# Masks made between the first graph's steps, a last group in two halves, and a longer wait before an input is turned

## The chip, the cores and the metric

The kernel runs on one core of a Trainium2 chip. The metric is the device time in microseconds of one execution. The profile's span, from the first to the last instruction, is a little shorter than that time.

## The reference

Eight graphs share one adjacency matrix of 2048 nodes; each node has 256 channels. For every graph the program computes masked attention in 8 heads of 32 channels, a feed-forward block, and three layer normalizations:

```python
qkv = x @ w_qkv                                    # (F=8, N=2048, 3*256)
scores = einsum('fnhd,fmhd->fhnm', q, k) / sqrt(32)
attn = softmax(where(adj > 0, scores, -1e9))
t = attn @ v
x1 = layernorm(x + t) * g1 + b1
f_out = relu(x1 @ w1 + b1) @ w2 + b2
ref = layernorm(x1 + f_out) * g2 + b2
out = layernorm(x + ref)
```

The adjacency is an int32 matrix in HBM.

## The kernel before, in words

A **graph** f has four chunks of 512 queries (qc), two groups of four heads (g) and 16 key blocks of 128 (mb). One **item** (f, qc, g, mb) is a key block against 512 queries in four heads; there are 1024 items, 128 for a graph, in the order of the loops f, qc, g, mb. A **group** is the 16 items of one (f, qc, g).

The main loop has a **step** t for each item. It lets the planner run (`advance(t)`), then emits the exponential of item t+1 on ACT (L237), the scores of item t+2 on PE with two additions of the mask on DVE (L230, L233), the values of item t on PE (L249), and `add_up`, which sums exponentials for the softmax denominators. Of the 16 tiles of exponentials of a group, POOL adds six to the first of its chain (L271), and six go by accumulating DMAs issued by POOL (`MOVED`, L268). `denominator` then multiplies the four sums by a block of ones on PE (L315). Scores use three pairs of PSUM banks in turn, values one bank; one more bank is left for all other work.

All other work runs as **generators in a list, sorted by a due time**. In one step at most one generator is given the free bank (`yield BANK`), and a matmul costs credit: 2200 credits come in each step and none are kept over, a projection's half costs 2048, a set of four transposes 1400. A generator that has said `MORE` or `WAIT` keeps the bank. `yield n` sleeps n steps. The generators are: `turn` (loads 512 rows of the next graph's x, L172, sleeps 5 steps, transposes them and stores the result to HBM, L177), `ask` and `project` (reload a transposed chunk, L196, and make queries, or keys and values), `denominator`, `outcome` (division by the denominators, L356, and adding x by a DMA), `tail` (normalizations, feed-forward, output). `NEXT` says at which step of a graph each starts. Inputs use a pool of three tiles, `take` and `give`.

**Masks.** Before the loop, `begin()` reads the adjacency in 16 blocks of 512x512 (qc, c), turns them with PE transposes into fp8 masks (0 or a large negative number, L145, L147) and stores them to HBM (`MD`, L148). After the blocks of qc = 0 and 1 it emits the scores of items 0 and 1; then it makes the blocks of qc = 2 and 3, and then the main loop starts. During the second group of each chunk, at its odd steps, `load_mask` brings the next chunk's masks back from HBM (L151).

**The end.** The very last group's denominators use more, shorter terms. After the last item, `finish` divides, and takes the four rows of the chunk in two interleaved halves (`half_rows`, L396 to L441) through the normalizations and the feed-forward block. A check of the sums (L836 to L848) follows.

An engine executes its instructions in the order in which they are emitted. SP issues the loads and stores; a wait of one of them holds the ones behind it.

Of the kernel before, what the change touches and what calls it, by code (L numbers as in the profile page):

```python
# [10 lines left out]
F32 = mybir.dt.float32  # L11
# [50 lines left out]
def fast_path(ctx, tc, cst, x, adj, out, RS):  # L62
# [62 lines left out]
    MK = {}  # L125
# [23 lines left out]

    def load_mask(f, qc, k):  # L150
        nc.sync.dma_start(words(mask_piece(f, qc, k)), MD[qc, k])  # L151
# [17 lines left out]
    def turn(f, c):  # L169
        yield INPUTS - 2  # L170
        xc, xT = take([P, TPC, C], F32), take([P, 2, CH], F32)
        nc.sync.dma_start(xc, x[f, c * CH:(c + 1) * CH, :].rearrange("(j p) c -> p j c", p=P))  # L172
        yield 5
        yield from turn_rows(xc, xT)
        give(xc)
        yield 1
        nc.sync.dma_start(XD[f][c], xT)  # L177
        XT[f, c] = xT
        give(xT)
# [39 lines left out]

    PT, O, OT, RC, DT = {}, {}, {}, {}, {}  # L220

    def scores(item):
        f, qc, g, mb = item
        pt = PT[item] = pp.tile([P, 4, CH], F32, name="p")
        ps2 = [score_pair() for _ in range(2)]

# [14 lines left out]
    def values(item):  # L241
        f, qc, g, mb = item
        grp = (f, qc, g)
        if mb == 0:
            i = state["side"]
            O[grp] = ps_x[i].tile([P, CH], F32, name=f"x{i}")
# [14 lines left out]
    ENDED = MB - 5  # L261
    SUM = 4

    def add_up(item):
        f, qc, g, mb = item
        for chain in MOVED:
            if mb in chain[1:] and not ((f, qc, g) == items[-1][:3] and mb >= ENDED):
                nc.gpsimd.dma_start(PT[f, qc, g, chain[0]], PT.pop(item), accum_op=ALU.add)  # L268
        if mb in POOLED[1:] and not ((f, qc, g) == items[-1][:3] and mb >= ENDED):
            first = PT[f, qc, g, POOLED[0]]  # L270
            nc.gpsimd.tensor_tensor(first, first, PT.pop(item), ALU.add)  # L271


# [23 lines left out]
    def denominator(f, qc, g, ready):  # L297
# [3 lines left out]
        if (f, qc, g) == items[-1][:3]:  # L301
            blocks = [POOLED[0], 11, 12, MOVED[0][0], 13, 14, MOVED[1][0], 15]
            late = {n: len(items) - k for n, k in ((2, 2), (3, 1), (4, 1), (5, 0), (6, 0), (7, 0))}
# [28 lines left out]
        start(begin, outcome(f, qc) if (f, qc) != (F - 1, NCK - 1) else finish(f, qc), begin)  # L332

    def outcome(f, qc):
# [4 lines left out]
        yield from divide(f, qc, y)  # L339
        nc.gpsimd.dma_start(y, xin, accum_op=ALU.add)  # L340
        begin = items.index((f, qc, 1, LAST)) + SUM + 2
        if (f, qc) == (F - 1, NCK - 2):
            xb = take([P, TPC, C], F32)
            nc.sync.dma_start(xb, xin)
            start(begin + 8, tail(f, qc, y, xin, 2, xb), begin + 11)
# [14 lines left out]
    def tail(f, qc, y, xin, per=1, xb=None):  # L360
# [6 lines left out]
        yield from norm(z, per)  # L367
# [28 lines left out]
    def half_rows(h, y, xr, xb, yT, hT, dst):  # L396
        own = slice(2 * h, 2 * h + 2)
        q = slice(2 * h * P, 2 * (h + 1) * P)
        y, xr, xb = y[:, own], xr[:, own], xb[:, own]
# [3 lines left out]

        nc.vector.tensor_tensor(y, y, xr, ALU.add)
        if h:
            yield
        found = half_stats(y)
        yield
# [3 lines left out]
        yield  # L412
        ps = bank()
        transposes(ps, [y[:, j, a * P:(a + 1) * P] for a in range(2) for j in range(2)])
        for a in range(2):
            nc.scalar.activation(yT[:, a, q], ps[:, a * 2 * P:(a + 1) * 2 * P], AF.Identity,
                                 bias=cst["be1c"][:, a:a + 1], scale=cst["g1c"][:, a:a + 1])
        yield
        ps = bank()
        for d in range(2):  # L420
            for a in range(2):
                columns(ps[:, d * 2 * P:(d + 1) * 2 * P], w1s[:, a, d * P:(d + 1) * P], yT[:, a, q], start=(a == 0), stop=(a == 1))
            nc.scalar.activation(hT[:, d, q], ps[:, d * 2 * P:(d + 1) * 2 * P], AF.Relu, bias=cst["b1s"][:, d:d + 1], scale=1.0)  # L423
        yield
        ps = bank()
        for j in range(2):
            for d in range(2):
                columns(ps[:, j * C:(j + 1) * C], hT[:, d, (2 * h + j) * P:(2 * h + j + 1) * P], w2s[:, d, :],
                        start=(d == 0), stop=(d == 1))
# [3 lines left out]
        yield  # L433
        half_norm(z, *found)
        yield
# [3 lines left out]
        yield  # L439
        half_norm(z, *found)  # L440
        nc.sync.dma_start(dst[:, own], z)  # L441

    def finish(f, qc):
        y = yp.tile([P, TPC, C], F32, name="y")
        xr, xb = state["rows"]
        yield from divide(f, qc, y)
        yT, hT = (work.tile([P, 2, CH], F32, name=n) for n in ("turned", "hT"))
        dst = out[f, qc * CH:(qc + 1) * CH, :].rearrange("(p j) c -> p j c", p=P)
        both = [half_rows(h, y, xr, xb, yT, hT, dst) for h in range(2)]
        while both:  # L450
            for e in list(both):
                if next(e, both) is both:
                    both.remove(e)
            yield 1
# [101 lines left out]

    def begin():
        todo = deque((qc, c) for qc in range(NCK) for c in range(NCK))
# [46 lines left out]
    state["side"] = 0  # L605
    for t, (f, qc, g, mb) in enumerate(items):
        if g == 1 and mb % 2 and (f + 1 < F or qc + 1 < NCK):
            load_mask(f + (qc + 1) // NCK, (qc + 1) % NCK, mb // 2)
        for what, *which in NEXT.get(t % FRAME, []):
# [4 lines left out]
        if t == len(items) - MB // 2:  # L614
            xr, xb = state["rows"] = [take([P, TPC, C], F32) for _ in range(2)]
            nc.sync.dma_start(xr, x[f, qc * CH:(qc + 1) * CH, :].rearrange("(p j) c -> p j c", p=P))
        if t == len(items) - 2:
# [17 lines left out]
        if t == len(items) - 3:  # L635
            start(t, denominator(f, qc, g, t), t)
# [245 lines left out]
```

## Time and profile before

| | |
|---|---|
| median of 3 runs | 3190.41 us (3189.46 to 3194.38) |
| the profiled execution | 3196.28 us, span 3194.5 us |
| mean granted TensorE clock | 0.987 |
| PE, DVE, ACT, POOL busy | 96%, 86%, 76%, 81% of the span |
| DMA | 589.46 MB, mean 185 GB/s |
| span by stage | first additions of masks at 60.1 us; the second step's additions at 98.7; graph 1 begins at 458.9, then graphs 1 to 7 take 391.7, 379.4, 381.2, 381.2, 381.2, 381.2 us, and the last 385.4 us to its last additions |

The stages are read from the starts of the DVE additions (L233) in the timeline, two for each item. A page's group line has the line, the engine, the operation, output and inputs, shapes and count, then busy time, the mean ns of one, and the idle time of the engine before them with what ended it. A PE that is shown busy isn't PE at its peak, since matmuls are pipelined. A line of the timeline has the start, the time taken, the engine, the line, the operation and its count, and in brackets the idle time before it and what ended it.

### The profile page before, as it was taken

Reading aid. Unit: us, or ns where it says so; the run is one execution under the profiler, and the core shown is the slowest. Engines: PE = TensorE matmul, PEld = TensorE weight load, DVE = VectorE, ACT = ScalarE, POOL = GpSimd, SP = SyncE. Lnnn points to the kernel's source line nnn. Section 1 sums busy time; section 2 is a strip of 40 time slices with the busy share of each in tenths; the row PEclk is TensorE's granted clock in tenths of the full one; section 3 lists DMA queues with packets and bytes.
Section 4 is the critical chain, followed back from the end, with each engine's and each line's share of the span. In section 5 each row is a group of like instructions: output and inputs, shape, how many; then the busy total and the mean of one; then the engine's idle time right before and its main releaser. Section 6 shows DMA issues by size and latency. Waiting matters only on the chain. (4 is left out here: it accounts for less than half of the span.)

```text
span 3194.5 us, 68226 instructions
## 1 busy us (share of the span) xinstructions
PE 3081.7 (96%) x28868; PEld 963.0 (30%) x28868; DVE 2749.6 (86%) x3139; ACT 2417.7 (76%) x1909; POOL 2593.3 (81%) x1361
## 2 busy tenths in 40 slices
PE   7899999999999999999999999999999999999985
PEld 4222333222332223332333323323233233332222
DVE  4798988888889988889988988988988888889985
ACT  3677778777787777788777788778778778777774
POOL 0578888788888888888888888888889788889875
PEclk8899999999999999999999999999999999999998
DMA  9688889788798888898888899888879788888872
GB/s 323 142 192 193 183 175 199 161 188 189 179 195 188 191 194 178 176 204 196 187 177 174 194 208 198 168 182 196 196 174 203 177 196 192 176 177 166 178 150 64
DMA packets 153096, 589.46 MB, mean 185 GB/s; under 512 B 15024, under 2 KB 67760, under 8 KB 103888
## 3 DMA queue, kind: packets, MB, share of 16 engines
q0 software_dynamic: 64128, 433.22, 68.8%
q1 hardware_dynamic: 87840, 150.50, 13.7%
q8 instruction: 228, 3.74, 0.4%
q10 hardware_dynamic: 816, 1.31, 0.1%
q14 instruction: 84, 0.69, 0.1%
HBM read 146.67 MB, written 37.75 MB: 58 GB/s over the span
## 5 line engine op out<-in xcount | busy, mean ns | idle before, releaser
L233 DVE TENSOR_TENSOR p<-s,mask 128x1024 f32<-128x1024 f32 x2048 | 2409.1, 1218 | 325.0 <-PE s L230 182.9
L237 ACT ACTIVATE p<-p 128x2048 f32<-128x2048 f32 x1024 | 1956.0, 1910 | 566.5 <-DVE p L233 481.1
L271 POOL TENSOR_TENSOR p<-p 128x2048 f32<-128x2048 f32 x382 | 1875.4, 4909 | 359.1 <-ACT p L237 358.8
L230 PE MATMUL s<-qT,kT 32*128 32x512 f32 x8192 | 1172.5, 642 | 44.2 <-DVE p L233 39.4
L249 PE MATMUL x<-p,v 128*32 128x512 f32 x8192 | 1093.5, 606 | 4.6 <-ACT p L237 4.6
L230 PEld LDWEIGHTS s<-qT,kT 32*128 32x128 f32 x8192 | 320.9, 183 | 671.3 <-DVE p L233 643.6
L268 POOL DMA_DIRECT2D p<-p x382 | 416.8, 1092 | 70.1 <-ACT p L237 46.4
L249 PEld LDWEIGHTS x<-p,v 128*32 128x32 f32 x8192 | 161.5, 108 | 784.0 <-issue 310.2
L315 PE MATMUL x<-p,halves 128*32 128x512 f32 x2080 | 269.9, 595 | 0.0
L54 PE MATMUL x<-in,wqkv 128*32 128x512 f32 x1888 | 245.7, 592 | 0.0
L290 ACT ACTIVATE y<-y,nb,rs 128x256 f32<-128x256 f32 x372 | 219.1, 591 | 6.1 <-POOL nb L287 5.9
L278 DVE BATCH_NORM_STATS2 st<-y 128x6 f32<-128x256 f32 x372 | 155.0, 417 | 1.8 <-POOL y L370 1.8
L54 PE MATMUL x<-turned,w1s 128*32 128x512 f32 x992 | 123.9, 593 | 0.0
L54 PE MATMUL x<-w2s,hT 128*32 128x256 f32 x2016 | 121.8, 382 | 0.0
L54 PEld LDWEIGHTS x<-wqkv,in 128*32 128x32 f32 x3584 | 102.2, 110 | 64.1 <-issue 55.9
L54 PE MATMUL x<-wqkv,in 128*32 128x128 f32 x3584 | 117.4, 273 | 0.0
L315 PEld LDWEIGHTS x<-p,halves 128*32 128x32 f32 x2080 | 67.9, 111 | 156.9 <-issue 155.5
L368 POOL TENSOR_TENSOR y<-y,g2r 128x1024 f32<-128x1024 f32 x31 | 101.6, 3278 | 6.4 <-ACT y L290 6.4
L54 PEld LDWEIGHTS x<-in,wqkv 128*32 128x32 f32 x1888 | 61.3, 110 | 141.3 <-issue 116.5
L284 POOL TENSOR_TENSOR rs<-rs,mhalf 128x4 f32<-128x4 f32 x93 | 96.3, 1035 | 7.8
L370 POOL TENSOR_TENSOR y<-y,be2r 128x1024 f32<-128x1024 f32 x30 | 94.6, 3155 | 0.4
L54 PEld LDWEIGHTS x<-w2s,hT 128*32 128x32 f32 x2016 | 65.9, 111 | 70.7 <-issue 38.5
(121 smaller groups left out, 1301.1 us busy)
## 6 DMA issues: line engine op xcount, KB each, us to landing
p<-p POOLq DMA_DIRECT2D x382, 1024.0 KB, 10.0
in<-xd SPq DMA_DIRECT2D x87, 512.0 KB, 8.9
mask<-md SPq DMA_DIRECT2D x248, 128.0 KB, 8.6
y<-in_x_dram POOLq DMA_DIRECT2D x61, 512.0 KB, 10.1
p<-in_adj_dram SPq DMA_DIRECT2D x16, 1024.0 KB, 9.3
out_dram<-y SPq DMA_DIRECT2D x31, 512.0 KB, 6.2
in<-in_x_dram SPq DMA_DIRECT2D x30, 512.0 KB, 10.6
xd<-in SPq DMA_DIRECT2D x28, 512.0 KB, 8.8
```

Source lines behind the costliest of these rows:

```text
L54: nc.tensor.matmul(out[r:r + D], lhsT[:, r:r + D], rhs, start=start, stop=stop)
L230: nc.tensor.matmul(ps2[half][:, j, :], KT[f, mb // TPC, g][r:r + D, (mb % TPC) * P:(mb % TPC + 1) * P], QT[f, qc, g][r:r + D, :], start=Tr ...
L233: nc.vector.tensor_tensor(pt[:, 2 * half:2 * half + 2, :], ps, MK[f, qc, mb // 2][:, mb % 2, None, :].to_broadcast([P, 2, CH]), ALU.add)
L237: nc.scalar.activation(PT[item], PT[item], AF.Exp, scale=1.0 / math.sqrt(D))
L249: nc.tensor.matmul(O[grp][r:r + D, :], V[f, mb // TPC, g][:, mb % TPC, r:r + D], PT[item][:, h, :], start=(mb == 0), stop=(mb == LAST))
L268: nc.gpsimd.dma_start(PT[f, qc, g, chain[0]], PT.pop(item), accum_op=ALU.add)
L271: nc.gpsimd.tensor_tensor(first, first, PT.pop(item), ALU.add)
L278: nc.vector.bn_stats(st, t[:, j, :])
L284: nc.gpsimd.tensor_tensor(rs, rs, cst["mhalf"], ALU.pow)
L290: nc.scalar.activation(t[:, j, :], t[:, j, :], AF.Identity, bias=nb[:, j:j + 1], scale=rs[:, j:j + 1])
L315: nc.tensor.matmul(ps[r:r + D, :], cst["halves"][:, g, :], term[:, h, :], start=(n == 0), stop=(n == len(blocks) - 1))
L368: nc.gpsimd.tensor_tensor(z, z, rows(cst["g2r"]), ALU.mult)
```

## The change

It has three parts.

1. `begin()` makes the masks of qc = 0 and 1 only. The masks of qc = 2 and 3 are made by 32 `mask_job` generators, one for 128 keys and 512 queries, started every 9/4 steps from step 2. Four buffers are lent for it: a kT tile, a v tile and the halves of a y tile; the halves of y are given up after the first jobs of qc = 3 have used them. A job loads its part of the adjacency (512 rows of 512 bytes), sleeps 3 steps, converts it on ACT, transposes it when it gets the bank, makes the mask on DVE and stores it. If a mask isn't made when `load_mask` wants it, the loop calls `advance(t0, finish=True)` until it is. The projections of graph 1 start later (`LATER`).
2. The last group (`ENDING`) takes its 512 queries as two halves of 256: its first 8 items run over all keys for the first half, two key blocks an item, the other 8 for the second half. Each half has its own `closing`, which does the denominators, division, normalizations and feed-forward of its 256 rows. In the last graph, the tails are started and ordered differently (`CALM`, the y of chunk 2 is added on DVE), and the last rows of x are loaded half a group earlier.
3. `turn` sleeps 7 steps instead of 5 between its load and the transposes.

```diff
+    MK, MADE, spare = {}, {(qc, b) for qc in range(2) for b in range(MB)}, deque()
+    def mask_job(n):
+        while not spare:
+            yield 1
+        part = spare.popleft()
+        qc, b = divmod(n + 2 * MB, MB)
+        col = part.bitcast(I32).rearrange("p (j m) -> p j m", j=TPC)
+        nc.sync.dma_start(col, adj[qc * CH:(qc + 1) * CH, b * P:(b + 1) * P].rearrange("(j p) m -> p j m", p=P))
+        yield 3
+        cv = part.bitcast(BF16)[:, 0:CH]
+        nc.scalar.copy(cv, part.bitcast(I32))
+        yield 1
+        yield BANK
+        ps = bank(BF16)[:, 0, :]
+        state["credit"] -= TURN // 2
+        for j in range(TPC):
+            nc.tensor.transpose(ps[:, j * P:(j + 1) * P], cv[:, j * P:(j + 1) * P], identb)
+        m = part[:, CH // 2:3 * CH // 4].bitcast(F8)
+        nc.vector.tensor_scalar(m.bitcast(I8), ps, 0.0, CODE, op0=ALU.is_le, op1=ALU.mult)
+        yield 1
+        nc.sync.dma_start(MD[qc, b // 2, :, b % 2 * P:(b % 2 + 1) * P], m.bitcast(I32))
+        MADE.add((qc, b))
+        yield 3
+        if n < MB or any(part is u for u in parts[0:2]):
+            spare.append(part)
...
-        yield 5
+        yield 7
         yield from turn_rows(xc, xT)
...
+    ENDING = (F - 1, NCK - 1, 1)
+    HQ = CH // 2
...
     def values(item):
+        if grp == ENDING:
+            h, k = divmod(mb, MB // 2)
+            if k == 0:
+                O[grp] = ps_x[state["side"]].tile([P, CH], F32, name=f"x{state['side']}")
+            for b in range(2):
+                m = 2 * k + b
+                for i in range(4):
...
     def add_up(item):
+        if item[:3] == ENDING:
+            h = mb // (MB // 2) * (MB // 2)
+            if mb - h in (2, 4):
+                nc.gpsimd.tensor_tensor(first, first, PT.pop(item), ALU.add)
+            elif mb - h == 3:
+                nc.gpsimd.dma_start(PT[f, qc, g, h + 1], PT.pop(item), accum_op=ALU.add)
+            return
...
+    CALM = (15, 0, 1)
...
         if (f, qc) == (F - 1, NCK - 2):
             xb = take([P, TPC, C], F32)
             nc.sync.dma_start(xb, xin)
-            start(begin + 8, tail(f, qc, y, xin, 2, xb), begin + 11)
+            yield from divide(f, qc, y)
+            yield 1
+            nc.vector.tensor_tensor(y, y, xb, ALU.add)
+            start(begin + 3, tail(f, qc, y, xin, 2, xb), begin + 18)
+            return
...
+    def closing(h):
+        own, part, t0 = slice(2 * h, 2 * h + 2), slice(h * HQ, (h + 1) * HQ), len(items) - MB // 2 * (2 - h)
+        terms = [(5, 6), (1, 7), (0, 7), (6, 8), (7, 8)]
+        yield BANK
+        ps = bank()
+        for n, (block, when) in enumerate(terms):
+            if n:
+                yield MORE
+            while state["now"] < t0 + when:
+                yield WAIT
+            term = PT.pop((*ENDING, block + h * MB // 2))
+            state["credit"] -= 4 * CH
...
+    LATER = {80: [], 100: [(project, 2, 0)], 104: [(project, 3, 0)], 108: [(project, 0, 1)], 112: [(project, 1, 1)],
+             116: [(project, 2, 1)], 120: [(project, 3, 1)]}
...
-        todo = deque((qc, c) for qc in range(NCK) for c in range(NCK))
+        todo = deque((qc, c) for qc in range(2) for c in range(NCK))
...
+    both = yp.tile([P, TPC, C], F32, name="y").rearrange("p j c -> p (j c)")
+    parts = [kp.tile([P, CH], F32, name="kT"), vp.tile([P, TPC, P], F32, name="v").rearrange("p j c -> p (j c)"),
+             both[:, 0:CH], both[:, CH:2 * CH]]
+    spare.extend(parts)
     for t, (f, qc, g, mb) in enumerate(items):
         if g == 1 and mb % 2 and (f + 1 < F or qc + 1 < NCK):
+            t0 = t
+            while not {((qc + 1) % NCK, b) for b in (mb - 1, mb)} <= MADE:
+                advance(t0, finish=True)
+                t0 += 1
             load_mask(f + (qc + 1) // NCK, (qc + 1) % NCK, mb // 2)
+        while n_mask < 2 * MB and t >= 2 + 9 * n_mask // 4:
+            start(t, mask_job(n_mask), 3 * MB - 2 + n_mask if n_mask < MB else 4 * MB - 2 + n_mask)
+            n_mask += 1
...
-        if t == len(items) - 3:
-            start(t, denominator(f, qc, g, t), t)
+        for h in range(2):
+            if t == len(items) - MB // 2 * (2 - h) + 4:
+                start(t + 1, closing(h), len(items) + h)
```

`closing` goes on from there as `half_rows` did, with a bank asked for before each set of transposes or matmuls.

## The prediction

> **What bounds the kernel now.** I read the page first, then the timeline of the start and of the end, then the waits and landings of the loads. The page's busy line and costliest groups:
>
> ```profile
> PE 3081.7 (96%) x28868; PEld 963.0 (30%) x28868; DVE 2749.6 (86%) x3139; ACT 2417.7 (76%) x1909; POOL 2593.3 (81%) x1361
> L233 DVE TENSOR_TENSOR p<-s,mask 128x1024 f32<-128x1024 f32 x2048 | 2409.1, 1218 | 325.0 <-PE s L230 182.9
> ```
>
> A step (one item) is scores on PE, two mask additions on DVE, exp on ACT, values on PE. A bare step is bound by the DVE pair: additions start 2.55 us apart. A step with 2048 credits of other matmuls is PE's own: 1.14 (L230) + 1.07 (L249) + 0.86, less overlap, 2.92 us. The windows show PE busy 379 of 381 us in a graph of the middle. So time is lost where this cadence breaks: at the start, in two late loads, at the end. The timeline of DVE over the start:
>
> ```profile
> 63.51 2.36 DVE L233 TENSOR_TENSOR p<-s,mask 128x1024 f32<-128x1024 f32 x2 [1.08 <-PE s L230]
> 65.78 1.28 DVE L582 TENSOR_SCALAR p<-p 128x1024 bf16<-128x1024 int32 x2
> ...
> 95.27 1.23 DVE L145 TENSOR_TENSOR in<-s,ones 128x1024 fp8e5<-128x1024 bf16 x1 [1.38 <-PE s L141]
> 98.70 2.35 DVE L233 TENSOR_TENSOR p<-s,mask 128x1024 f32<-128x1024 f32 x2 [2.21 <-PE s L230]
> ```
>
> From 65.8 to 96.5 us only the masks of the last two query chunks are made; no step runs. The loads, from the page (KB each, median us from issue to landing) and from the view of line L172 (who waited for it; landings):
>
> ```profile
> q0 software_dynamic: 64128, 433.22, 68.8%
> q1 hardware_dynamic: 87840, 150.50, 13.7%
> ...
> p<-p POOLq DMA_DIRECT2D x382, 1024.0 KB, 10.0
> ...
> mask<-md SPq DMA_DIRECT2D x248, 128.0 KB, 8.6
> ```
>
> ```profile
>   PE x L95: 7.6, 2
> ...
> DMA to landing us min/median/max: 3.9/10.8/22.6
> ```
>
> q0 carries the accumulations that POOL issues, six per group of 16 steps; in the first group from the issue at 111.4 us to some 10 us after the last at 135.9: 35 us of a group's 47. q1 is SP's.
>
> **What the skill says.** "DMA: Bandwidth & Descriptors", section Queues, rings and completion order: each DMA engine goes round between the queues that have work, a packet at a time. The trace agrees. A q0 packet lasts 0.688x16x3194.5/64128 = 0.55 us in the mean (about 0.62 for the 8 KB ones, since small ones are counted in), a q1 packet 0.137x16x3194.5/87840 = 0.08. An input's load of 512 KB is 512 rows of 1 KB, 32 packets an engine: beside a busy q0, 32x0.70 = 22 us, and the longest took 22.6. A mask's load of 128 rows is 8 packets: 5.6 plus some 2 us fixed; measured 8.6. "PSUM — Partial Sum Buffer", section Engine vs sequencer instructions: the queues of ACT, DVE and POOL are strict FIFO. The trace agrees: at 3099 us ACT idled 5.60 us before a normalization that needed POOL's nb, with the next exp behind it.
>
> **The change, part by part.**
>
> *Start.* Eight of 16 mask blocks leave it. The third pair of additions starts when PE has its scores, about 66.2 instead of 98.7: **-33 us** (32.5, and a first step that PE ran at half clock, 3.9 us). Eight adjacency loads go too; nothing before 57 us changes, where PE is the bound.
>
> *The jobs' work.* 32 jobs of 128 keys x 512 queries: a load, an ACT copy (nearest row 0.58 us), four transposes, a 128x512 DVE operation from PSUM, a 64 KB store. The nearest step holds four transposes and L356's 0.68:
>
> ```profile
> 199.17 2.35 DVE L233 TENSOR_TENSOR p<-s,mask 128x1024 f32<-128x1024 f32 x2
> 201.44 0.68 DVE L356 TENSOR_TENSOR y<-x,rc 128x512 f32<-128x512 f32 x1
> 202.04 2.34 DVE L233 TENSOR_TENSOR p<-s,mask 128x1024 f32<-128x1024 f32 x2
> ```
>
> 2.87 us against 2.55: 0.31 a job. 25 jobs in ordinary steps: **+8** (5 to 15: less if the 16-bit source halves the DVE time, more where a displaced projection doubles up later, 0.86 instead of 0.37). ACT has 0.6 us idle a step and covers its copy.
>
> *The jobs' loads.* Each is 512 rows of 512 B: as many packets as the input's load, 32 an engine, so 22 us when issued early in a burst of accumulations. The copy is emitted 3 steps later; SP runs ahead by up to a step, so cover is 8 to 11 us. A copy that waits stands on ACT before the next exp, and PE's values wait for that; slack there is about 1 us (the exp of 117.55 ended at 119.46, its values began at 120.88, less 0.58 for the copy). SP issues each load behind the previous job's store, which waits for DVE, and after the part's old store has landed. The bursts cover about steps 5-17, 20-33, 36-48, 52-66, 68-81, 84-97. By the planner's rules job 3 loads at 8 and copies at 11; jobs 9-11 at 25-27 and 28-30; job 16 at 44 and 47; job 21 at 57 and 60; job 23 at 77 and 80; job 25 at 85 and 88. One stall empties the backlog, since stopped steps issue no more accumulations: q0's two or three outstanding transfers drain in 10 to 16 us (8 packets each, 0.65 with ours between). I take landing less cover: 6 + 7 + 2.5 + 8 + 0.5 + 6 = **+30**. Bounds: 8 (all near the median landing 10.8) and 60 (ten us in each of six bursts).
>
> *The jobs' order.* Only two of four parts return after job 15, so from job 20 on two jobs run per round of 8 steps, plus delays for a bank. By due times, job 21's transposes (due 83) wait from step 61 to 73 behind the first tail's matmuls (due 63), a denominator and a division. Jobs 23, 24 load at 77, 78, 25, 26 at 85, 86; masks of the fourth chunk are wanted two at a time at steps 81 to 95, job 25 at 89, 27 at 91, 29 at 93, 31 at 95. So the main loop has to advance the planner without scores: 2 advances at step 89, 8 at 91, 14 at 93, 20 at 95. In 91 a load (4 to 12 us), a copy, a transpose and a DVE operation stand before the next scores, with w1, w2 and POOL's 2.67 + 2.66 us for y between them: about 16 us instead of 2.9. In 93 jobs 29 and 30, a normalization through POOL, four v parts: about 16. In 95 job 31: +6. In 89: +2. That is 34; 18 units of pulled-forward fill at 0.37 each are saved later, 7: **+27** (10 to 40).
>
> *Two steps more.* In the second graph two transposes wait, at steps 49 and 61: additions 7.8 and 7.6 us apart instead of 2.9. The page's DMA row has these loads at 10.6 median; the two took 19 and 21 us. 5 steps are 14.5 us, 7 are 20: **-10** (0 to -10). The two slots are held 2 steps longer; the loads queue behind them on SP, with no step in a later graph shown waiting, so nothing is added.
>
> *Projections four steps later, masks' parts in kT and v buffers, y added on DVE for chunk 2 of the last graph.* 0 each; the same matmuls, all due after step 125, lie beside steps; DVE's addition (1.4 us) replaces a DMA. A late projection would show as more than 3.1 us between additions at 120 to 134.
>
> *Last group.* Now, last exp to end:
>
> ```profile
> 3143.07 1.91 ACT L237 ACTIVATE p<-p 128x2048 f32<-128x2048 f32 x1 [0.44 <-DVE p L233]
> ...
> 3160.84 1.09 ACT L394 ACTIVATE y<-y,nb,rs 128x256 f32<-128x256 f32 x2 [11.99 <-issue]
> ```
>
> The exp ends at 3145.0, the span at 3194.5: 49.5 us. The aim needs the first half's closing to be over by then. It is not: its denominator may begin at step 6 of the group, but w1 and w2 of chunk 2's tail (due 1015 against 1024) hold the bank in steps 5 to 9, so its five terms take steps 10 to 14 and its reciprocals step 15. Division, norm, w1, w2 follow the last values (1.1): 0.6 + 3.9 + 0.9 + 1.3 + 1.7 + 3 + 2 = 14 us; only then come the second half's denominators, 5x0.86 = 4.3, and its whole chain, about 30. Together 49 (45 to 55): no gain. The POOL wait at 3099 (additions 10.2 us apart) should shrink, since the norms come 4 steps earlier and the last group has 4 POOL additions instead of 6: **-3** (-12 to +6).
>
> **Sum.** -33 + 8 + 30 + 27 - 10 - 3 = +19 us against the profiled execution's own 3196.3. That lies 5.9 above the runs' median of 3190.4, to which I apply the same sum: **3209**.
>
> **Rivals.** *Loads land in time (faster).* If landings stay near the median and the bursts don't catch them, the loads cost 8 and forced steps 10: -33 + 8 + 8 + 10 - 10 - 3 = -20, 3170. For it: the first loads go out in the quiet start, and no tail's accumulation stands beside them before step 39. Against: half of the 28 input loads took over 10.8 us, and these have the same packets. It decides where mean stalls per burst fall under about 2 us and the four forced steps under 17 in all. *The DMA engines become the bound (much slower).* 32 jobs add 640 packets of about 0.03 us (a 1 KB packet's share of the mean, by size), 1.1 us of 16 engines, 35 in all, to a share of 0.83 in steps 0 to 75; then accumulations land later, p buffers run short and every burst stalls fully: 60 + 40 instead of 57: +62, 3252. Against: small packets fit in the gaps. *The halves do overlap.* If the first half's chain hid under the last steps, the end would shrink by some 12: 3197. Against: the due times above.
>
> **Numbers.** A difference under 0.2%, 6.4 us, can't be told from none. Forecast 0.52 (0.02 of it within 0.2%); DMA-bound 0.10; loads in time 0.25; halves overlapping 0.13, at the edge: 0.03 faster, 0.07 same, 0.03 slower. That gives slower 0.50 + 0.10 + 0.03 = 0.63, same 0.09, faster 0.28. Range: the unknown costs run from 8 + 10 to 60 + 40 and the end from -12 to +6; leaving out a tenth on either side gives 3160 to 3250. The likeliest case's own range is 3195 to 3245.
>
> **What would show it.** Right: third pair of additions near 66 us; ACT copies of the parts waiting for the adjacency load, 5 to 10 us about once a group of the first 96 steps; gaps over 10 us between additions near steps 91 and 93; no transposes waiting for an input in graph 2; last exp to end still near 49 us. Wrong: adjacency loads landing in under 9 us in the bursts, no gap over 5 us at steps 89 to 95, or an end of under 40 us.

## The result, and the profile after

The changed kernel takes 3232.62 us (median of 4 runs, 3227.48 to 3234.77), the kernel before in the same job 3189.93 (4 runs). The ratio is 1.0126, 95% interval 1.011 to 1.0142: slower by 42.7 us, where +19 was forecast. The profiled execution took 3234.77 us, its span 3232.9: 38.4 more than the span before, whose profiled execution lay 5.9 us above its own median.

The page of the changed kernel, busy line, queues and the two groups that answer to those shown of before:

```profile
PE 3101.6 (96%) x29220; PEld 973.6 (30%) x29220; DVE 2755.1 (85%) x3154; ACT 2425.1 (75%) x1934; POOL 2588.7 (80%) x1358
L276 DVE TENSOR_TENSOR p<-s,mask 128x1024 f32<-128x1024 f32 x2016 | 2372.7, 1219 | 327.4 <-PE s L273 198.1
...
q0 software_dynamic: 63696, 430.60, 67.6%
q1 hardware_dynamic: 102944, 150.50, 13.7%
...
mask<-md SPq DMA_DIRECT2D x248, 128.0 KB, 8.5
```

These lines hardly move: the same additions at the same 1.22 us each, nearly the same bytes on the queues. q1's packets grew by 15,104. Nothing in the totals says where 40 us went; the cadence does. The DVE timeline of the changed kernel over the start:

```profile
59.78 2.36 DVE L276 TENSOR_TENSOR p<-s,mask 128x1024 f32<-128x1024 f32 x2 [1.32 <-PE s L273]
...
66.66 2.36 DVE L276 TENSOR_TENSOR p<-s,mask 128x1024 f32<-128x1024 f32 x2 [1.08 <-PE s L273]
```

The third pair starts at 66.66 instead of 98.70. That gain is given back in steps 89 to 96 of the first graph, in the DVE timeline:

```profile
340.33 0.69 DVE L167 TENSOR_SCALAR kT<-x 128x512 int8<-128x512 bf16 x1 [0.53 <-issue]
345.10 2.36 DVE L276 TENSOR_TENSOR p<-s,mask 128x1024 f32<-128x1024 f32 x2 [4.08 <-PE s L273]
349.11 2.36 DVE L276 TENSOR_TENSOR p<-s,mask 128x1024 f32<-128x1024 f32 x2 [1.66 <-PE s L273]
363.49 0.69 DVE L600 TENSOR_TENSOR y<-x,y 128x512 f32<-128x512 f32 x1 [12.02 <-PE x L54]
...
369.05 2.36 DVE L276 TENSOR_TENSOR p<-s,mask 128x1024 f32<-128x1024 f32 x2 [2.42 <-PE s L273]
372.14 2.36 DVE L276 TENSOR_TENSOR p<-s,mask 128x1024 f32<-128x1024 f32 x2 [0.73 <-PE s L273]
...
387.35 2.36 DVE L276 TENSOR_TENSOR p<-s,mask 128x1024 f32<-128x1024 f32 x2 [1.30 <-PE s L273]
389.86 2.35 DVE L276 TENSOR_TENSOR p<-s,mask 128x1024 f32<-128x1024 f32 x2 [0.15 <-PE s L273]
...
399.06 2.36 DVE L276 TENSOR_TENSOR p<-s,mask 128x1024 f32<-128x1024 f32 x2 [1.30 <-PE s L273]
```

Between additions at 349.1 and 369.1, 372.1 and 387.4, 389.9 and 399.1 only fill runs: DVE idles 12.02 us for a feed-forward matmul, and makes masks (L167). That is the main loop forcing the planner so that the jobs end. When the jobs come first (*due_first*, below), the gaps at steps 90 to 95 are gone. Who waited for the jobs' loads, in the view of line L156 of the changed kernel (us, times), and the loads' landings:

```profile
  ACT v L159: 13.0, 4
  ACT y L159: 9.6, 3
...
DMA to landing us min/median/max: 2.7/6.5/15.3
```

Seven copies stood 22.6 us on ACT. By ACT's timeline three of these waits lie in the gaps between additions ahead of step 88: 3.03 us in that at step 14 (5.4 us from one step's additions to the next), 5.75 at step 32 (9.2) and 7.00 at step 63 (10.7). The inputs' loads, in the view of line L197, where before PE had waited 7.6 and 5.0 us:

```profile
  PEld L165: 0.8, 1
...
DMA to landing us min/median/max: 4.5/10.5/23.5
```

No turn waits any more, although the slowest load still takes 23.5 us. The last graph holds what the forecast didn't have. DVE there, in chunk 1:

```profile
2915.00 2.36 DVE L276 TENSOR_TENSOR p<-s,mask 128x1024 f32<-128x1024 f32 x2 [0.27 <-PE s L273]
2921.61 0.43 DVE L345 BATCH_NORM_STATS2 st<-y 128x6 f32<-128x256 f32 x1 [4.25 <-DMA y<-in_x_dram]
2922.07 0.18 DVE L346 BATCH_NORM_AGGREGATE mv<-st 128x2 f32<-128x6 f32 x1
2922.17 0.40 DVE L345 BATCH_NORM_STATS2 st<-y 128x6 f32<-128x256 f32 x1
2922.60 0.18 DVE L346 BATCH_NORM_AGGREGATE mv<-st 128x2 f32<-128x6 f32 x1
2922.70 2.34 DVE L276 TENSOR_TENSOR p<-s,mask 128x1024 f32<-128x1024 f32 x2
```

The tail begins 7 steps after the results instead of 10. Its statistics stand on DVE ahead of the additions and wait 4.25 us for the transfer that adds x to y; the additions are 7.7 us apart. Later in the graph, same view:

```profile
2969.61 2.36 DVE L276 TENSOR_TENSOR p<-s,mask 128x1024 f32<-128x1024 f32 x2 [0.37 <-issue]
2971.89 0.42 DVE L345 BATCH_NORM_STATS2 st<-y 128x6 f32<-128x256 f32 x1
...
2973.93 0.18 DVE L346 BATCH_NORM_AGGREGATE mv<-st 128x2 f32<-128x6 f32 x1
2974.03 2.35 DVE L276 TENSOR_TENSOR p<-s,mask 128x1024 f32<-128x1024 f32 x2
```

Four row blocks' statistics in one step fill DVE from 2971.89 to 2974.1: a step of 4.4 us. The end, on ACT:

```profile
3181.98 1.91 ACT L280 ACTIVATE p<-p 128x2048 f32<-128x2048 f32 x1 [0.35 <-DVE p L265]
...
3227.46 1.09 ACT L466 ACTIVATE y<-y,nb,rs 128x256 f32<-128x256 f32 x2 [4.00 <-DVE nb L464]
```

The last exp ends at 3183.9, 49.0 us before the end of the span (49.5 before).

Counted from where each step's additions start in the two traces, changed less before (running total in brackets): start to step 4, -32.0 (-32.0); steps 4 to 88, +22.1 (-9.8); steps 88 to 100, +40.4 (+30.6); rest of the first graph and second graph, -11.1 (+19.5); five graphs in the middle, +2.3 (+21.8); last graph, +17.4 (+39.2); end, -0.7 (+38.4).

### The profile page after: what moved, and what is told of

It reads as the page before. It is cut to its first block, busy times and chain, and to the rows that moved or that the text cites. A ratio compares the mean times of both kernels' runs of the same rounds, so it can differ in the third digit from the quotient of the medians.

```text
span 3232.9 us, 69092 instructions
## 1 busy us (share of the span) xinstructions
PE 3101.6 (96%) x29220; PEld 973.6 (30%) x29220; DVE 2755.1 (85%) x3154; ACT 2425.1 (75%) x1934; POOL 2588.7 (80%) x1358
## 3 DMA queue, kind: packets, MB, share of 16 engines
q10 hardware_dynamic: 816, 1.31, 0.1%
## 5 line engine op out<-in xcount | busy, mean ns | idle before, releaser
L276 DVE TENSOR_TENSOR p<-s,mask 128x1024 f32<-128x1024 f32 x2016 | 2372.7, 1219 | 327.4 <-PE s L273 198.1
L336 POOL TENSOR_TENSOR p<-p 128x2048 f32<-128x2048 f32 x378 | 1839.0, 4865 | 379.0 <-ACT p L280 378.2
L307 PE MATMUL x<-p,v 128*32 128x512 f32 x8064 | 1083.5, 610 | 10.3 <-ACT p L280 8.4
L333 POOL DMA_DIRECT2D p<-p x378 | 402.4, 1066 | 69.8 <-ACT p L280 40.8
L379 PE MATMUL x<-p,halves 128*32 128x512 f32 x2016 | 261.1, 592 | 0.2 <-DVE kT L167 0.2
L54 PE MATMUL x<-turned,w1s 128*32 128x512 f32 (+1 forms) x1008 | 127.2, 603 | 2.2 <-ACT hT L587 0.8
L54 PEld LDWEIGHTS x<-wqkv,in 128*32 128x32 f32 x3584 | 102.1, 110 | 63.5 <-issue 53.8
## 6 DMA issues: line engine op xcount, KB each, us to landing
p<-p POOLq DMA_DIRECT2D x380, 1024.0 KB, 10.1
in<-in_x_dram SPq DMA_DIRECT2D x30, 512.0 KB, 10.3
p<-in_adj_dram SPq DMA_DIRECT2D x8, 1024.0 KB, 13.4
```

The costliest lines, as they stand in the source:

```text
L54: nc.tensor.matmul(out[r:r + D], lhsT[:, r:r + D], rhs, start=start, stop=stop)
L276: nc.vector.tensor_tensor(pt[:, 2 * half:2 * half + 2, :], ps, MK[f, qc, mb // 2][:, mb % 2, None, :].to_broadcast([P, 2, CH]), ALU.add)
L307: nc.tensor.matmul(O[grp][r:r + D, :], V[f, mb // TPC, g][:, mb % TPC, r:r + D], PT[item][:, h, :], start=(mb == 0), stop=(mb == LAST))
L379: nc.tensor.matmul(ps[r:r + D, :], cst["halves"][:, g, :], term[:, h, :], start=(n == 0), stop=(n == len(blocks) - 1))
```

## The experiments

Ratios to the kernel before are of runs on the same chip in the same job.

| kernel | us, median | ratio, 95% interval | span | first graph | last graph |
|---|---|---|---|---|---|
| before | 3189.9 | | 3194.5 | 398.8 | 385.4 |
| changed | 3232.6 | 1.0126 (1.011 to 1.0142) | 3232.9 | 429.5 | 402.8 |
| tails_old | 3215.6 | 1.0049 (1.0033 to 1.0065) | 3216.3 | 428.7 | 380.9 |
| begin_ten | 3225.1 | 1.0098 (1.0081 to 1.0115) | 3225.1 | 425.6 | 397.4 |
| single_rows | 3222.5 | 1.0095 (1.008 to 1.0111) | 3221.2 | 429.5 | 386.6 |
| due_first | 3212.2 | 1.0041 (1.0027 to 1.0054) | 3211.3 | 407.3 | 402.4 |
| masks_start | 3203.5 | 1.0026 (1.0019 to 1.0032) | 3201.7 | 397.3 | 403.7 |
| only_seven | 3186.4 | 0.9958 (0.9943 to 0.9974) | 3184.2 | 397.3 | 385.8 |
| best_start | 3185.2 | 0.9974 (0.9962 to 0.9986) | 3180.1 | 397.2 | 381.1 |
| rows_2k | 3232.5 | 1.0121 (1.01 to 1.0141) | 3228.8 | 423.4 | 402.9 |
| half_calm | 3176.1 | 0.9952 (0.9938 to 0.9965) | 3174.3 | 382.5 | 380.9 |
| half_busy | 3174.0 | 0.9949 (0.9936 to 0.9963) | 3171.9 | 384.4 | 381.3 |
| calm_twenty | 3174.9 | 0.9952 (0.9938 to 0.9965) | 3174.7 | 383.6 | 381.0 |
| half_three | 3189.3 | 0.9985 (0.9978 to 0.9991) | 3187.7 | 399.6 | 380.8 |
| half_six | 3178.2 | 0.9949 (0.9932 to 0.9967) | 3176.1 | 389.2 | 381.6 |

A graph's length runs from its first addition to the next graph's first (the last graph's to its last addition). In a first graph whose masks are made ahead, the break of 35 us for them is inside it. Medians of different rows come in part from different chips: in these jobs the kernel before had medians of 3189.9 to 3195.1 us. So a difference of two rows is given by the medians, by the spans of the two profiled executions or by the ratios, and these differ by several us.

**The last graph's tails.** *tails_old* gives chunks 0 and 1 of the last graph their old tails:

```diff
-        if f == F - 1:
-            start(begin + 7, tail(f, qc, y, xin, 2), begin + 18)
-        else:
-            start(begin + 10, tail(f, qc, y, xin), begin + 26)
+        start(begin + 10, tail(f, qc, y, xin), begin + 26)
...
-        while xb is None and f == F - 1 and state["now"] % MB not in CALM:
-            yield 1
```

> Two of the changed kernel's edits undone, for chunks 0 and 1 of the last graph alone: their tails start 10 steps after begin with the normalizations one row block a step, as before, and no wait for a calm step. Theory A, that these tails cost what the sum left out (the last graph took 402.8 us instead of 385.4): the last graph falls to 386 to 390, the time to 3215 to 3220, and the 7.7 us between additions at its step 45 goes. Theory B, that the two halves of the last group or the later positions of the inputs cost it: the last graph stays near 400 and the time within 5 us of 3232.6.

The last graph fell from 402.8 to 380.9, further than theory A had it, and the gap at step 45 went. The end after the last addition is 2.1 us longer (54.4 instead of 52.3), so graph and end together are 19.8 us shorter. The time fell by 17.0 us by the medians, 16.6 by the spans, 25 by the ratios: these edits cost some 20 us. In DVE's timeline of tails_old one row block's statistics stand in a step, and the additions keep their 2.8 us:

```profile
2929.67 2.33 DVE L276 TENSOR_TENSOR p<-s,mask 128x1024 f32<-128x1024 f32 x2
2931.93 0.41 DVE L345 BATCH_NORM_STATS2 st<-y 128x6 f32<-128x256 f32 x1
...
2932.48 2.36 DVE L276 TENSOR_TENSOR p<-s,mask 128x1024 f32<-128x1024 f32 x2
```

With the old tails the last graph is 4.5 us shorter than before the change and its end 1.4 longer: what is left of the change there (last group, chunk 2's tail) gains 3.1. To split the cost, *begin_ten* changes only `begin + 7` to `begin + 10`:

> The changed kernel, with the tails of chunks 0 and 1 of the last graph begun 10 steps after the results instead of 7; their two row blocks a step and their stop until a quiet step stay as changed. In the trace the last graph is 22 us shorter with all of the old tails. Theory A (the early start costs only the one wait in which the normalization's statistics stand on VectorE ahead of the additions while y's accumulation is still landing, 7.7 us at step 45 against a regular 2.9; the rest is the four additions' worth of work put in one step): the gap at step 45 goes, the gaps of 4.4 us and the 7.2 at step 105 stay, last graph 396 to 399, 3226 to 3229 us. Theory B (the early start moves all of the tail to steps that TensorE has full, and the row blocks in one step are hidden): the last graph falls by 15 or more, to 388 or below, 3217 us or less.

The gap at step 45 went, the others stayed; last graph 397.4, -5.4. Theory A held, with a time just under its range. *single_rows* also takes one row block a step:

```diff
-            start(begin + 7, tail(f, qc, y, xin, 2), begin + 18)
+            start(begin + 10, tail(f, qc, y, xin), begin + 18)
```

> The changed kernel with the last graph's tails of chunks 0 and 1 begun after 10 steps and with one row block a step in their first and last normalizations and in the second one too; what is left of their change is the stop until a quiet step and their due time. Against the version that only begins after 10 steps (3225.1, last graph 397.4 us, with six gaps of 4.4 to 7.2). Theory A (two to four row blocks in one step put 1.0 to 1.7 us of statistics on VectorE and 1.2 to 2.4 us of ACT in front of a step's additions and exponentials, which are then late): the gaps go but for one or two, last graph 381 to 386, 3209 to 3214. Theory B (the stop until a quiet step piles the transfers and the next chunk's tail on each other, and costs what is left): last graph 393 or more, 3221 or more.

Last graph 386.6, another -10.8; two gaps are left (8.3 at step 105, 4.9 at 123), as theory A had it, and the graph is 0.6 us longer than its range. The time was not in it: it fell only from 3225.1 to 3222.5, and the two intervals overlap. In the profiled executions the first graph, which the edit doesn't touch, was 3.9 us longer, and the end after the last addition 3.4 longer (55.1 instead of 51.7): a part of the gain in the graph comes back there. Graph and end together split into 6.0 us for the early begin, 7.4 for row blocks put together, 6.4 for the stop until a quiet step with the earlier due time (the rest, not run alone). Each is one trace against another, and by the times alone the second can't be told from nothing.

**The jobs' order.** *due_first* makes a job due when it is queued:

```diff
-            start(t, mask_job(n_mask), 3 * MB - 2 + n_mask if n_mask < MB else 4 * MB - 2 + n_mask)
+            start(t, mask_job(n_mask), n_mask)
```

> The changed kernel with one number changed: a mask job's due time is its own number, so it gets the bank ahead of everything else. By the planner's rules the forced advances fall from 44 (steps 89 to 95) to 2 (step 95). Theory A, that the jobs' order costs what the additions show between steps 88 and 100 (40 us): graph 0 falls from 429.5 to 390 to 397 and the time to 3193 to 3200. Theory B, that the wait is the loads' own (the accumulations beside them) and only moves: the same 40 us turn up as stalls of about 10 us in the other groups, time over 3215.

The span of the third chunk's 32 steps fell from 130.9 to 97.9 us: -33, the forced steps. But chunks 0 and 1 grew from 93.3 and 105.9 to 100.1 and 107.3, and the fourth from 99.4 to 102.1, with eleven small gaps; net -22.2 in the first graph, -20.4 in the time by the medians (27 by the ratios). Between the theories: the order costs 33 of the 40 us that theory A gave it, and jobs that go first bring stalls of their own.

**Masks inside the loop or ahead of it.** *masks_start* makes all masks before the loop, without jobs, their buffers and the later projections, the rest as changed:

```diff
-        todo = deque((qc, c) for qc in range(2) for c in range(NCK))
+        todo = deque((qc, c) for qc in range(NCK) for c in range(NCK))
```

> The changed kernel with all masks made ahead of the loop again, no mask jobs, projections as before; last group, tails and the 7 steps as in the changed kernel. Theory A (the jobs cost 62 us in graph 0 against 32 saved ahead of it): first to third pair of additions 39 us, graph 0 near 398 from its first addition, time 3200 to 3204. Theory B, that moving the masks is a gain and the loss lies in the other parts: time over 3235.

3203.5: made inside the loop as the change does it, the 32 masks cost a net 29 us by the medians (31 by the spans, 32 by the ratios), start's gain included. Theory A held.

**Two steps more.** *only_seven* is the kernel before with `yield 7`:

> The kernel before with 7 steps instead of 5 between an input's load and its transposes, nothing else. Theory A: the two waits of graph 1 go (its 391.7 us become 381), other graphs unchanged, 3179 to 3181. Theory B, that the two tiles held for two steps more delay the queries and projections behind them: graph 1 gains 10 but graphs 2 to 6 lose a few us each, 3185 to 3195.

The second graph went from 391.7 to 379.4 us, the third from 379.4 to 381.4, the other graphs stayed within 1.5 us, and the span fell by 10.3. The waits went as theory A had it, and of theory B's losses in the later graphs only those 2.0 us came, but the median of 3186.4 lies above theory A's 3179 to 3181; by the ratio it is 13 us under the kernel before. *best_start* takes masks_start with the old tails:

> The changed kernel with all masks made ahead of the loop, and the last graph's tails of chunks 0 and 1 as before: of the change are left the seven steps for an input, the last group by 256 queries, and chunk 2's tail. Against the version with seven steps alone (3186.4 us, profiled span 3184.2) it prices the last group. Theory A (the two costs found so far add up: 29 us for the masks inside the loop, 17 for the tails): 3232.6 - 29 - 17 = 3186, and by the traces 3201.7 - 22 + 2 = 3182 of span, so 3181 to 3187, the last graph at 381 and last addition to end near 55. Theory B (with both out of the way the last group's halves show a gain of their own, their later tails no longer crowded): 3176 or below. Theory C (they collide elsewhere): 3190 or more.

3185.2, within theory A's 3181 to 3187; last graph 381.1, last exp to end 51.0 us. Against only_seven its span is 4.1 us less and its ratio 0.0016 more, with overlapping intervals: the last group by 256 queries can't be told from no change.

**What a job's stall depends on.** *rows_2k* reads a job's 256 KB as 128 rows of 2 KB instead of 512 of 512 bytes. It leaves out the right choice of the block, so the masks of chunks 2 and 3 are those of other parts of the adjacency; the instructions are otherwise the same:

```diff
-        nc.sync.dma_start(col, adj[qc * CH:(qc + 1) * CH, b * P:(b + 1) * P].rearrange("(j p) m -> p j m", p=P))
+        nc.sync.dma_start(part.bitcast(I32), adj[b * P:(b + 1) * P, qc * CH:(qc + 1) * CH])
```

> The changed kernel with each job's load taken as 128 rows of 2 KB instead of 512 rows of 512 bytes: the same bytes in a quarter of the rows; it reads other blocks of the adjacency than the masks need, so the masks of chunks 2 and 3 are those of other blocks, and nothing else differs. Theory A (the stalls at steps 14, 32 and 63, and part of those at 90 to 96, are ACT and TensorE waiting for a load whose 32 packets a DMA engine come one between each two of an accumulating transfer): with 8 packets an engine the load lands within its three steps, the gaps at 14, 32 and 63 go and those at 90 to 96 shrink, 12 to 25 us off: 3208 to 3221. Theory B (the loads wait for the bytes that the queues move, not for their packets, or the gaps have another cause): gaps as before, within 5 us of the changed kernel. If the forced steps alone cost what they do, without any wait for a load, the gaps at 90 to 96 stay whole and only the three earlier ones go, -15.

3232.5 against 3232.6. The gaps at 32 and 63 stayed (9.4 and 8.3 us). The gap at step 14 went, but not by the edit: the copy there waited 2.88 us as against 3.03, and the gap is also missing in tails_old, begin_ten and single_rows, whose loads are those of the changed kernel. The view of the load's line in rows_2k (L155 there):

```profile
  ACT v L158: 13.4, 5
  ACT y L158: 11.4, 3
...
DMA to landing us min/median/max: 2.9/6.1/16.9
```

A quarter of the rows (12,288 packets fewer on q1), and much the same waits and landings: the number of the load's own packets, on which the forecast rested, is not what stalls a job. One more execution of this kernel is *rows_due*:

> The changed kernel with the loads of 128 rows of 2 KB (reading other blocks of the adjacency than the masks need) once more, one look, to see whether the gaps of the run before recur at the same steps. Both theories: as in that run, gaps at the same steps within 2 us each.

They recurred at 32 and 63, 9.5 and 9.4 us (3230.7 us, one run); the gap at step 52 (4.4) did not.

*half_calm* and *half_busy* keep 16 jobs (chunk 3) in the loop, due at once, old tails, loads only in four of 16 planned steps, copies a step apart:

```diff
-        while not spare:
+        while not spare or state["now"] % MB not in (2, 3, 4, 5):   # half_busy: (8, 9, 10, 11)
             yield 1
...
-        yield 3
+        yield 3 + n % 4
```

> Chunk 2's masks made ahead of the loop, chunk 3's 16 by jobs inside it, due at once; a job's load is issued only in steps 2 to 5 of each 16 (four jobs a time, their copies one step apart), the last graph's tails as before. Measured in the traces so far: the accumulating transfers fill the DMA engines from step 7 of 16 to step 0 of the next (busy 0.8 to 1.0) and leave them in steps 2 to 6. Theory A (jobs stall because their loads land while the accumulations fill the engines): no gap over 5 us in the first graph; against all masks ahead (3185.2) half of the 33 us of the start is saved and 16 jobs' work of 0.25 us each is added, 3185 - 16.5 + 4 = 3173, so 3170 to 3176. Theory B (a job stalls wherever its load is issued, about 1 us a job as with all jobs due at once, 42 us for 32 less 8 of work): 3173 + 16 = 3189.

> As the version with loads in the quiet steps, but the loads are issued only in steps 8 to 11 of each 16, while the accumulating transfers fill the DMA engines. Theory A: each group of four loads shows a gap of 5 to 10 us in which ACT's copies wait for the load, four such groups, 10 to 25 us slower than with the quiet steps. Theory B: within 4 us of it.

3176.1 and 3174.0. The sum of 3173 for half_calm nearly held, and the planned busy steps cost nothing more, but the pair does not compare what it was meant to. half_calm's SP queue, in the timeline:

```profile
162.23 1.20 SPq L156 DMA_DIRECT2D kT<-in_adj_dram  x1
163.52 1.32 SPq L156 DMA_DIRECT2D v<-in_adj_dram  x1
164.93 10.84 SPq L156 DMA_DIRECT2D y<-in_adj_dram  x2
```

The planner put these four loads at step 34; SP issued them at steps 30 and 31 and finished issuing at 35, since their parts had long been free. A place in the program's order is no place in time on a queue with nothing to wait for. So half_calm's loads went out beside full DMA engines after all (share 0.96 at 126 to 131 us, 1.04 at 162 to 176, 1.06 at 199 to 221), and half_busy's in no busier ones (0.86, 1.00 and 0.64 at 137, 170 and 227 us). Neither kernel shows a gap over 5 us after the start, and their loads in kT and v are issued 11 to 33 us ahead of their copies: with so much time, loads beside full engines stalled nothing here. *half_three* and *half_six* test that: no gate on steps, and three or six steps from load to copy, which is all that differs between them.

> Chunk 2's masks ahead of the loop, chunk 3's 16 by jobs due at once, the tails as before, as in the two versions with four loads a time, but each load is issued as soon as its part is free, and the copy comes three steps after it, as in the changed kernel. Theory A (a job stalls when the time from its load's issue to its copy, 7 to 14 us in the changed kernel since the load waits for the store of the same part's last mask, is shorter than the 6 to 17 us that the load takes; the two versions with four loads a time had 11 to 33 us and no stall): the gaps of the version with all jobs due at once come back in the first 40 steps (6.4, 4.4, 4.7, 6.1, 4.7 there, 11 us over the regular steps), 3184 to 3189. Theory B (half the jobs are few enough for the DMA engines, whatever the slack): no gap over 5 us, 3173 to 3178.

> The same with six steps from a load to its copy instead of three, nothing else. Theory A: about 17 us of slack or more, no gap over 5 us, 3173 to 3177, 8 to 14 us below the version with three steps. Theory B: the same time as with three steps, within 3 us.

3189.3 against 3178.2: 11.1 us for three steps of slack, as theory A had it (half_six's own time is 1 us above its range). Who waited for the jobs' loads in half_three (view of line L156), and the landings:

```profile
  ACT y L159: 9.0, 3
  ACT v L159: 6.1, 1
  ACT kT L159: 4.1, 1
...
DMA to landing us min/median/max: 2.9/7.2/20.0
```

and in half_six:

```profile
  ACT y L159: 3.7, 1
  ACT v L159: 1.6, 1
...
DMA to landing us min/median/max: 4.1/7.0/21.3
```

The loads land no sooner; the copies come later, and ACT's wait falls from 19.2 us to 5.3. How one wait reaches DVE, in half_three's timeline:

```profile
121.70 2.34 DVE L276 TENSOR_TENSOR p<-s,mask 128x1024 f32<-128x1024 f32 x2
128.04 0.69 DVE L167 TENSOR_SCALAR v<-x 128x512 int8<-128x512 bf16 x1 [4.00 <-PE x L165]
130.11 2.35 DVE L276 TENSOR_TENSOR p<-s,mask 128x1024 f32<-128x1024 f32 x2 [1.37 <-PE s L273]
```

ACT's copy waits, so the transposes on PE wait, with the next scores behind them, so the mask operation on DVE waits: 8.4 us between additions. half_three had four more gaps than the start's (8.4, 5.6, 4.5, 8.6), half_six one (7.2).

Last, *calm_twenty* has 20 jobs and one 512 by 512 block less ahead of the loop than half_calm:

> The version with loads in the quiet steps with 20 jobs instead of 16: one block of 512 by 512 less ahead of the loop, four jobs more, which only the two parts that outlive step 56 carry, at steps 66 and 82. Theory A: 33/8 = 4.1 us less at the start against 1 us of work, 2 to 4 us faster than with 16 jobs. Theory B (the later steps have no room for a job, or their masks come so late that the steps are forced): the same or slower, with a gap near steps 90 to 96.

3174.9 against 3176.1, intervals over each other: theory A's 2 to 4 us don't show. Its first loop steps begin earlier (third pair at 79.9 against 84.2), and it loses as much by the end of the second graph, which is 386.8 long against 385.2.

The best versions, half_busy, half_calm, calm_twenty and half_six, stand 0.5% below the kernel before, and below only_seven by less than the intervals tell apart.

## Why the prediction was right or wrong

**Start: right.** -33 forecast, -32.0.

**Jobs' work and loads: size off, reason partly wrong.** 38 forecast, +22.1 up to step 88: 16.6 in the three gaps over the regular 2.9 us a step (30 forecast for the loads), 5.5 for the rest (8 for the work; DVE's mask operation took 0.69 us, as long as L356's with its f32 source). The chain was right (load late, ACT's copy stands, PE and DVE behind it), and it hit near steps that were named (gaps at 14, 32 and 63); where exactly a gap falls is in part chance, since tails_old, begin_ten and single_rows, with the same first graph, have theirs at 30 and 31, at 49 or 51, and at 63. What failed is the term of 22 us for "as many packets as the input's load, 32 an engine": the slowest load took 15.3 us, not 22, and with 8 packets an engine the stalls were much the same. The Trainium skill, "DMA: Bandwidth & Descriptors", section Queues, rings and completion order, does not carry that count: it speaks of packets of about 9 to 17 descriptors, where a packet of this trace is one row. How many rows an engine takes at a turn no run here shows. The runs put slack in the term's place: three steps of cover are short for a load that takes 3 to 20 us, and six steps are nearly enough.

**Jobs' order: right in kind and place, 13 too small.** 27 forecast, +40.4. The gaps (additions apart, from the DVE timeline) are 8.3, 19.9, 15.2 and 9.2 us at steps 90, 92, 94 and 96, 41 over the regular 2.9 each; forecast 34 gross. Step 89 was given 2 and cost 5.4, step 91 was given 13 and cost 17.0; steps 93 and 95, given 13 and 6, cost 12.3 and 6.3. In the longest gap no load was waited for: ACT's copies of the parts at 361.3 us follow its operations of the feed-forward block at once. In the last, ACT's copy waited 4.04 us for its load. The 7 us of saved fill did not come back: from step 100 to the end of the first graph the change is -0.2, and the second graph's -10.9 is the two inputs' gain. A part of what was missed is a clock that the working counted once, at the start, and nowhere else. PE in the timeline of the changed kernel, before and after the stop of step 89:

```profile
336.71 1.07 PE L307 MATMUL x<-p,v 128*32 128x512 f32 x8
...
339.85 0.38 PE L165 MATMUL x<-identb,kT 128*128 128x128 bf16 x4 [1.75 <-DVE v L167]
341.08 1.93 PE L54 MATMUL x<-in,wqkv 128*32 128x512 f32 x8 [0.84 <-DVE kT L167]
342.94 2.09 PE L273 MATMUL s<-qT,kT 32*128 32x512 f32 x8
344.96 1.94 PE L307 MATMUL x<-p,v 128*32 128x512 f32 x8
346.67 1.31 PE L54 MATMUL x<-in,wqkv 128*32 128x512 f32 x8
347.90 1.14 PE L273 MATMUL s<-qT,kT 32*128 32x512 f32 x8
```

Between 338.1 and 341.1 us PE worked 0.38 us; then eight scores took 2.09 us instead of 1.14, eight values 1.94 instead of 1.07, a projection's matmuls 1.93 instead of 1.04 and the next 1.31. That is 0.89 + 0.95 + 0.87 + 0.27 = 3.0 of the 6.5 us that this stop (5.4) and the slow step behind it (4.0 instead of 2.9, so 1.1) cost. The windows give a granted clock of 0.50 from 340.4 to 347.2 us, and 0.50 too from 156.1 to 162.8 and from 251.7 to 258.4, behind the loads' stalls at steps 32 and 63. The Trainium skill has it in "TensorE: Matmul & The Clock Gate", section Part 1: PE's clock goes to half after about one idle window of 3.4 us and comes back after a busy one; this trace agrees in kind, and its lengths are 3.0 us of near idleness and 6.8 us at half. Such a stop of PE is paid twice here: once as the wait, once as the slow start behind it.

**Two steps more: right.** -10 forecast. Alone (*only_seven*) the second graph is 12.3 us shorter and the third 2.0 longer, -10.3 in the span; here they are 10.9 shorter and 1.8 longer. The later projections cost nothing, as forecast (-0.2 from step 100 to 128).

**Last group: the end right, the graph ahead of it wrong, and this is the step that failed.** The last exp to the end was forecast at 49 and is 49.0: the halves don't overlap. What the term "Last group" counted came too: with the old tails (*tails_old*) the additions 10.2 us apart at step 116, the POOL wait that was to shrink because chunk 2's "norms come 4 steps earlier", are gone, and graph and end gain 3.1 us, where -3 was forecast. But the tails of chunks 0 and 1 were changed as well (begun after 7 steps, two row blocks a step and four in the second normalization, a stop until a quiet step), and the sum gave them nothing, without a reason. Together they cost 17 (the medians) to 25 us (the ratios), 19.8 in the last graph and the end, shown by undoing them; so this term measured +16.7 instead of -3. Much of it was in the page of before: y's transfer takes 10.1 us in the median from issue, and a step that PE fills (2.92 us) leaves DVE beside its additions (2.36) about half a microsecond, where four blocks of statistics take 2.2.

Errors by span: +13 (order), +20 (last graph and end), -16 (loads and work), +2 (middle graphs, of which 1.8 is the third graph's), together +19 on the forecast of +19. That the miss is 19 us and not 35 is luck: the loads were priced too high by a wrong count, and this hid nearly half of what was priced too low. (In the working for the last group the seven terms said to make 14 us make 13.4, which changes nothing.)

**The rivals.** Loads in time: refuted by 22.6 us of waits. DMA engines as the bound: with the jobs' work it needed 108 us for loads and order, 62.5 were found, and the accumulating transfers land in 10.1 us in the median as against 10.0 before, where this rival has them land later. Halves overlapping: refuted by the end.

**Left open.** What makes one load take 3 us and another 20 was not settled: it is not the number of its packets, and the planned step of its issue could not test it, since SP doesn't keep to the plan. The stop until a quiet step was not run alone. The forced steps were not run apart from the jobs' order: *due_first* removes most of them and brings small stalls in their place.

## What to carry to other kernels

Work moved from a start into a loop's idle slots saves the start only if the loop gives each piece its slack, as half_three and half_six show with 11.1 us between them: count the time from a load's issue (which waits for the buffer's old store) to its first use against the slowest landing in the trace, not the median, and give deadlines early enough that nothing is forced. A diff's least spoken-of edits need a price too: three steps' earlier begin, two and four row blocks a step and a stop, in a loop whose engines are full, cost some 20 us, more than half of the 32 that the main edit saved at the start. Where statistics of side work stand in one queue with the main loop's operations, try them one to a step and look at the end as well: here the last graph then lost 10.8 us and the end gained 3.4.

## What the runs showed of the hardware

- A stop of some 3 us with almost no matmul was followed by 6.8 us at half clock inside the running loop (granted 0.50 from 340.4 to 347.2 us; 3.0 us lost after the stop at 338 us), not only at the kernel's start.
- A job's load landed no sooner with fewer and longer rows here: 512 rows of 512 bytes landed in 2.7/6.5/15.3 us (least, median, most), 128 rows of 2 KB in 2.9/6.1/16.9, the same 256 KB each.
- A DMA issue on SP is not always short. The median is 0.38 us for a job's load in a kT or v part of the changed kernel, but in half_calm two such issues together took 10.84 us at 164.9 and 16.63 us at 204.1, and the next issue on SP came only behind them. Over both stretches the windows show the 16 DMA engines fully busy (share 1.06 and 1.03). That the one causes the other was not tested.
- The SP queue ran up to seven steps (some 20 us) ahead of the program's plan where nothing held it: half_calm's loads that were planned at step 50 were issued at 43 to 45.
